# A deformable convolution's samples: 128x128 matmuls against two 64x64 tiles of TensorE

## The chip, the cores and the metric

The kernel runs on one core of one Trainium2 chip. The metric is the device time of one execution in microseconds (us); before the change three runs gave 6296.52 to 6303.05, median 6301.44.

## What is computed

Four layers follow one another on an array of 4 x 128 x 128 x 128 in fp32. Each adds its result to its input, and each input is group-normalised first. The change is in the first, a deformable 3x3 convolution with four groups of 32 channels:

```python
offset = jnp.einsum('bchw,oc->bohw', x, w_off) + b_off[None, :, None, None]
...
py = off[:, :, :, 0] + (ky - PAD).reshape(1, 1, K * K, 1, 1) + jnp.arange(H, dtype=jnp.float32).reshape(1, 1, 1, H, 1)
...
val = gather(y0i, x0i) * (wy0 * wx0)[:, :, None]
val = val + gather(y0i, x0i + 1) * (wy0 * wx1)[:, :, None]
val = val + gather(y0i + 1, x0i) * (wy1 * wx0)[:, :, None]
val = val + gather(y0i + 1, x0i + 1) * (wy1 * wx1)[:, :, None]
wg = w.reshape(COUT, G, CG, K * K)
return jnp.einsum('bgckhw,ogck->bohw', val, wg)
```

For every output pixel, group and tap, an offset of its own moves the place that the tap reads; the value there is a bilinear mix of four pixels. The other three layers (a scan of 1-D convolutions over rows, a message layer, a triangle product) are not touched.

## The kernel before, in words

`deform_layer` works on blocks of 3 output rows (RY), 43 per image, 172 in all. Within a block, columns are taken 4 at a time (RX): 32 column blocks. The kernel relies on offsets smaller than one pixel in size (a general version stands by for larger ones and isn't run here), so, with each tap counted at the place that it looks at, the samples around 3 x 4 places all lie in a patch of 5 x 6 = 30 pixels (NS). A bilinear mix is then a product: samples = patch x weights, where the weight of a patch pixel is a tent in y times a tent in x.

The partition dimension of that product carries 4 groups x 30 pixels = 120 lanes (LANES). The patch, `pixels`, is a block-diagonal matrix: lanes of group g have values in the 32 channels of group g alone, zeros elsewhere (the tiles are cleared once, before the loops, and the loads write only the diagonal). Three steps make one block:

- `spread_offsets` (L465, matmul L488): the two tents of every lane, from offsets split into three bf16 parts. `spread` holds the stationary matrices, 25 rows x LANES columns, for 10 phases. They stand four times, at partitions 0, 32, 64 and 96, so that these matmuls run on tiles of 32 rows x 128 columns. One tap takes 9 matmuls (three rows of 130 columns for y, six for x of 96 or 3 columns); taps come in pairs, 5 slots per block (SLOTS), into the PSUM tiles `t_ps`.
- `tents` (L494): ScalarE copies the y half out of PSUM (L497), VectorE multiplies it with the x half into `m` (L498), fp32, LANES x 9 taps x 3 rows x 130 columns.
- `sample` (L500, matmul L507): for each of four column blocks, `pixels` is stationary (120 x 128, fp32) and 27 rows of 4 columns of `m` are moving, 108 columns; the result, 128 channels x 108, goes to `v_ps`. `keep_samples` copies four of them at a time to `v` (L518). The last column block has two columns more (162).

`convolved` (L556, matmul L567) then applies the 3x3 taps as 15 matmuls of 128x128 weights over 128 to 384 columns, accumulating in `conv_ps`; `finish` (L540) adds the input and stores.

All orders are written by hand: `manual_schedule` (L656) makes each engine run its instructions in the order in which the code issues them. A block's loop has 8 steps (L676 to L689), and in each TensorE gets: lane matmuls of the next block if the table DONE asks for them (5 of 8 steps), two or three matmuls of the convolution (7 of 8), four sample matmuls, and a piece of side work from `step` (transposes L365 and offset matmuls L380 for rows that come later). Lane matmuls use 32-row tiles; everything else uses the whole array.

Loads stand on SP's queue: `load_places` (offsets), `load_pixels` (L453, four per block, one for each group, each 30 partitions), and x for the side work. The end block of each image has an extra row, done with narrow samples (`me`, 12 columns).

An fp32 matmul is two weight loads and two passes on TensorE; the profile counts each.

Of the kernel before, what the change touches and what calls it, by code (L numbers as in the profile page):

```python
# [21 lines left out]
NG = 4  # L22
NK = 9
NL = NK * NG
CG = P // NG
# [13 lines left out]
RY, RX = 3, 4  # L39
SY, SX = RY + 2, RX + 2  # L40
NS = SY * SX
LANES = NS * NG
NXB = S // RX
NG_X = NXB // 4
NYB = S // RY + 1
# [137 lines left out]
def deform_layer(tc, c, small, x, w_off, b_off, w_def, x1, tabs, offs):  # L183
# [9 lines left out]
    nc = tc.nc  # L193
# [3 lines left out]
    with ExitStack() as ctx:  # L197
# [22 lines left out]
        NPY, NPX = RY + 1, RX + 2  # L220
        NPH = NPY + NPX
        spread = wp.tile([P, NPH, LANES], BF16, name="spread")
        nc.vector.memset(spread, 0.0)
# [11 lines left out]
        with tc.tile_pool(name="l0prep", bufs=1) as prep:  # L235
            mask = prep.tile([NG, LANES], F32, name="mask")
            nc.vector.memset(mask, 1.0)
            nc.gpsimd.affine_select(
                out=mask, in_=mask, pattern=[[1, LANES]], compare_op=ALU.is_ge,
                fill=0.0, base=0, channel_multiplier=-NS,  # L240
            )
            nc.gpsimd.affine_select(
                out=mask, in_=mask, pattern=[[-1, LANES]], compare_op=ALU.is_ge,
                fill=0.0, base=NS - 1, channel_multiplier=NS,
            )
            awayi = prep.tile([NG, NPH, LANES], I32, name="awayi")
            for i in range(NPY):
                nc.gpsimd.iota(
                    awayi[:, i], pattern=[[0, NG], [1, SY], [0, SX]], base=-1 - i,
                    channel_multiplier=0,  # L250
                )
            for i in range(NPX):
                nc.gpsimd.iota(
                    awayi[:, NPY + i], pattern=[[0, NG * SY], [1, SX]], base=-1 - i,
                    channel_multiplier=0,
                )
            away = prep.tile([NG, NPH, LANES], F32, name="away")
            nc.vector.tensor_copy(away, awayi)
            at = {}
            for v in (-1, 0, 1):  # L260
                at[v] = prep.tile([NG, NPH, LANES], F32, name=f"at_{v + 1}")
                nc.vector.tensor_scalar(at[v], away, float(v), None, ALU.is_equal)
            kinds = prep.tile([NG, 3, NPH, LANES], F32, name="kinds")
            nc.vector.tensor_tensor(kinds[:, 0], at[0], at[-1], ALU.subtract)
            nc.vector.tensor_tensor(kinds[:, 1], at[1], at[-1], ALU.add)
            nc.vector.scalar_tensor_tensor(
                kinds[:, 1], at[0], -2.0, kinds[:, 1], ALU.mult, ALU.add
            )
            for i in range(2):
                nc.vector.tensor_tensor(  # L270
                    kinds[:, i], kinds[:, i],
                    mask.unsqueeze(1).to_broadcast([NG, NPH, LANES]), ALU.mult,
                )
            nc.vector.tensor_copy(kinds[:, 2], at[0])
            kinds16 = prep.tile([NG, 3, NPH, LANES], BF16, name="kinds16")
            nc.vector.tensor_copy(kinds16, kinds)
            for q in range(4):
                p0 = 32 * q
                nc.sync.dma_start(spread[p0 : p0 + 1], kinds16[0:1, 2])
                for g in range(NG):  # L280
                    for kind in range(2):
                        for n in range(NSPLIT):
                            p1 = p0 + 1 + g * NPART + kind * NSPLIT + n
                            nc.sync.dma_start(spread[p1 : p1 + 1], kinds16[g : g + 1, kind])


            zrow = prep.tile([NXB, 2 * SX * P], F32, name="zrow")
            nc.vector.memset(zrow, 0.0)
            zoff = prep.tile([2 * NL, NPART, 2 * OW], BF16, name="zoff")
            nc.vector.memset(zoff, 0.0)  # L290
            for b in range(B):
                t = tabs[b].rearrange("x (r s) c -> x r s c", s=SX)
                nc.scalar.dma_start(
                    t[0:NXB, 0:2].rearrange("x r s c -> x (r s c)"), zrow
                )
                nc.scalar.dma_start(
                    t[0:NXB, S + 2 : S + 3].rearrange("x r s c -> x (r s c)"), zrow[:, 0 : SX * P]
                )
                for r0 in range(0, S, NXB):
                    nc.scalar.dma_start(  # L300
                        t[0:1, 2 + r0 : 2 + r0 + NXB, 0:2].rearrange("x r s c -> (x r) (s c)"),
                        zrow[:, 0 : 2 * P],
                    )
                rows_ = offs[b].rearrange("(p n) l -> p n l", n=NPART)
                nc.scalar.dma_start(rows_[:, :, 0 : 2 * OW], zoff)
                nc.scalar.dma_start(rows_[:, :, (S + 2) * OW :], zoff)
# [146 lines left out]
        def load_pixels(b, j):  # L453
            t = pixels[(b * NYB + j) % 2]
            for g in range(NG):
                nc.sync.dma_start(
                    t[g * NS : (g + 1) * NS, :, g * CG : (g + 1) * CG],
                    tabs[b][0:NXB, RY * SX * j : RY * SX * j + NS, g * CG : (g + 1) * CG].rearrange(
                        "x l c -> l x c"
                    ),  # L460
                )
            return t
# [37 lines left out]
        def sample(m, pix, i, rows):  # L500

            n = rows * RX
            vp = ps_v.tile([P, 4 * n + 2 * rows], F32, name="v_ps")
            for h in range(4):
                xb = 4 * i + h
                w = RX + 2 if xb + 1 == NXB else RX
                nc.tensor.matmul(  # L507
                    vp[:, h * n : h * n + rows * w].rearrange("p (k c) -> p k c", c=w),
                    lhsT=pix[0:LANES, xb, :], rhs=m[:, :, RX * xb : RX * xb + w],
                    start=True, stop=True,  # L510
                )
            return vp

        def keep_samples(vp, v, i, rows):
# [144 lines left out]
        load_row(0)  # L659
        load_row(1)  # L660
        pixel_tiles = {0: load_pixels(*blocks[0])}
        for i in range(NB_):
            multiply(advance(i + 1))
        vps, before, convs, stats = None, None, iter(()), None
        for n, (b, j) in enumerate(blocks):
            load_row(n + 2)
            if n + 1 < len(blocks):
                pixel_tiles[n + 1] = load_pixels(*blocks[n + 1])
            pix = pixel_tiles.pop(n)
            m = ms.pop(n).rearrange("p k r c -> p (k r) c")  # L670
# [47 lines left out]
        while step(B, S):  # L718
# [10 lines left out]
            most_ps, lhsT=most, rhs=c.ident[0 : 2 * NL, 0 : 2 * NL], start=True, stop=True  # L729
# [852 lines left out]
@with_exitstack  # L1582
def tile_preact_convs(ctx: ExitStack, tc: tile.TileContext, x, w_off, b_off, w_def, w_conv,
                      wself_T, wm_T, wk_T, *rest):
    nc = tc.nc
    *w3, out = rest
    cpool = ctx.enter_context(tc.tile_pool(name="consts", bufs=1))
    small = ctx.enter_context(tc.tile_pool(name="small", bufs=1))
    dram = ctx.enter_context(tc.tile_pool(name="dram", bufs=1, space=DRAM))
    c = make_consts(nc, cpool)  # L1590
    imgs = [
        dram.tile([PADW * NG * PADW, 4 * CG], F32, name=f"img_{b}") for b in range(B)
    ]
    tabs = [dram.tile([NXB + 1, (S + 3) * SX, P], F32, name=f"tab_{b}") for b in range(B)]
    offs = [
        dram.tile([2 * NL * NPART, (S + 4) * OW], BF16, name=f"off_{b}") for b in range(B)
    ]
    x1 = dram.tile([B, S, S, S], F32, name="x1")
    x2T = dram.tile([B, P, S, S], F32, name="x2T")
    x3d = dram.tile([B, P, S, S], F32, name="x3d")  # L1600
    gates = dram.tile([B, P, S, S], F32, name="gates")
    norms, far = deform_layer(tc, c, small, x, w_off, b_off, w_def, x1, tabs, offs)
    with tc.If(nc.values_load(far, min_val=0, max_val=1) > 0):
        deform_general(tc, c, norms, x, w_off, b_off, w_def, x1, imgs)
    counted = scan_layer(tc, c, small, x1, w_conv, norms, x2T)
    message_and_triangle(tc, c, x2T, x3d, gates, counted, (wself_T, wm_T, wk_T), w3, out)
# [45 lines left out]
```

## Time and profile before

| what | value |
|---|---|
| median of three runs | 6301.44 us |
| the profiled execution's own time | 6289.25 us |
| its span, first to last instruction | 6287.5 us |
| mean granted TensorE clock | 0.934 |
| first and last sample matmul (L507) | 222.7 and 3753.4 us |
| sample matmuls, `m` / `me` | 11,008 / 256 passes |
| lane matmuls L488 | 14,016 weight loads |
| convolution L567 | 5,160 passes |

PE is TensorE's matmul row and PEld its weight-load row; loads overlap matmuls, and the recorded duration of a matmul includes its latency, so the distance from one start to the next says more of the pace than the duration does. DVE is VectorE, ACT ScalarE, POOL GpSimd, SP the engine that issues most DMAs. In a group line the columns are: line, engine, operation, tiles and shapes, count, busy us, mean ns of one, idle us before it and what ended that idle time. A form such as 120*128 is the stationary operand, rows by columns. PEclk is the granted share of TensorE's clock in tenths.

### The profile page before, as it was taken

How to read it: one execution, taken by the hardware profiler on the slowest of the kernel's cores; microseconds unless marked ns; L12 is line 12 of the kernel's file. 1: busy time of each engine (PE TensorE's matmuls, PEld its weight loads, DVE VectorE, ACT ScalarE, POOL GpSimd, SP SyncE). 2: the span in 40 equal slices, each digit the busy share in tenths (PEclk: the TensorE clock that was granted, in tenths of full speed). 3: DMA queues.
4: the chain of work that ended last, by engine and by line, in shares of the span. 5: the costliest groups of instructions: out<-in, count | busy, mean ns of one | idle time of the engine just before them, and what ended most of it. 6: DMA issues, size and time to landing. Idle time of an engine off the chain costs nothing. (4 is left out here: it accounts for less than half of the span.)

```text
span 6287.5 us, 117915 instructions
## 1 busy us (share of the span) xinstructions
PE 5392.4 (86%) x45160; PEld 4669.4 (74%) x45160; DVE 3346.1 (53%) x10388; ACT 2803.2 (45%) x5848; POOL 762.4 (12%) x660
## 2 busy tenths in 40 slices
PE   0588999899898998989999998999879679688697
PEld 0477878788777787777888888999838458466586
DVE  5353434354344454443333338999964665656656
ACT  0334444344444444444444432333254574564655
POOL 0111111001111101111000001222200100200102
PEclk9989999899999999999999998999989899899898
DMA  2445545445454444545333422323230521612514
GB/s 88 103 123 118 122 112 122 111 102 126 113 115 117 102 123 118 117 113 117 80 71 74 79 54 85 95 84 92 81 141 29 216 102 46 223 54 91 196 45 153
DMA packets 1112274, 668.36 MB, mean 106 GB/s; under 512 B 718933, under 2 KB 985366, under 8 KB 1095318
## 3 DMA queue, kind: packets, MB, share of 16 engines
q1 hardware_dynamic: 1101906, 655.37, 38.7%
q8 instruction: 361, 5.91, 0.4%
q10 hardware_dynamic: 9796, 5.34, 0.3%
q14 instruction: 211, 1.73, 0.1%
HBM read 380.24 MB, written 280.03 MB: 105 GB/s over the span
## 5 line engine op out<-in xcount | busy, mean ns | idle before, releaser
L498 DVE TENSOR_TENSOR m<-ty,t_ps 120x390 f32<-120x390 f32 x1548 | 804.8, 557 | 1788.2 <-ACT ty L497 1787.7
L507 PEld LDWEIGHTS v_ps<-m,pixels 120*128 120x128 f32 x11008 | 1439.0, 199 | 86.8 <-issue 12.0
L507 PE MATMUL v_ps<-m,pixels 120*128 120x108 f32 (+1 forms) x11008 | 1484.8, 280 | 2.6 <-ACT v L523 1.7
L567 PE MATMUL conv_ps<-v,wdef 128*128 128x128 f32 (+2 forms) x5160 | 1336.6, 386 | 12.1 <-DVE x1c L540 7.6
L518 ACT COPY v<-v_ps 128x432 f32<-128x432 f32 x1376 | 704.0, 512 | 1331.3 <-PE v_ps L507 1329.0
L567 PEld LDWEIGHTS conv_ps<-v,wdef 128*128 128x128 f32 x5160 | 834.1, 197 | 172.5 <-issue 28.9
L497 ACT COPY ty<-t_ps 120x390 f32<-120x390 f32 x1560 | 686.0, 486 | 376.1 <-PE t_ps L488 367.6
L488 PEld LDWEIGHTS <-spread 25*120 25x120 bf16 x14016 | 500.9, 143 | 266.0 <-issue 199.5
L488 PE MATMUL t_ps<-places,spread 25*120 25x96 bf16 (+2 forms) x13932 | 582.2, 247 | 83.3 <-DVE m L498 62.7
L1429 PEld LDWEIGHTS proj_ps<-wcat,X 128*128 128x128 f32 x4096 | 474.5, 192 | 27.4 <-issue 27.4
L1429 PE MATMUL proj_ps<-wcat,X 128*128 128x128 f32 x4096 | 483.8, 275 | 0.6
L386 POOL TENSOR_TENSOR off<-off,koff 72x512 f32<-72x512 f32 x128 | 162.1, 1267 | 2538.8 <-DVE off L383 2510.2
L1047 PE MATMUL m_ps<-carry,w 128*128 128x172 f32 x2286 | 361.3, 310 | 0.0
L1034 ACT ACTIVATE rowT<-x1T_ps,t_x,s_x 128x128 f32<-128x128 f32 x512 | 192.7, 457 | 366.4 <-PE x1T_ps L1027 363.6
L1510 POOL TENSOR_TENSOR work<-work,gate 128x512 f32<-128x512 f32 x128 | 165.0, 1293 | 1571.6 <-ACT work L1509 1435.2
L1047 PEld LDWEIGHTS m_ps<-carry,w 128*128 128x128 f32 x2286 | 345.5, 188 | 0.0
L1435 DVE TENSOR_TENSOR L<-proj_ps,work 128x256 f32<-128x256 f32 x256 | 155.0, 606 | 347.9 <-ACT work L1433 347.9
L1114 POOL TENSOR_TENSOR sum_h<-sum_h,x2c 128x512 f32<-128x512 f32 x128 | 162.6, 1270 | 1351.8 <-DVE x2c L1111 1351.8
L1433 ACT ACTIVATE work<-proj_ps 128x512 f32<-128x512 f32 x256 | 152.8, 597 | 298.1 <-PE proj_ps L1429 298.1
L365 PE MATMUL img_ps<-ident,xin 128*128 128x128 f32 x512 | 94.2, 315 | 196.2 <-DMA xin<-in_x_dram 193.4
L1522 PE MATMUL out_ps<-outw,work 128*128 128x128 f32 x1024 | 210.0, 307 | 48.9 <-POOL work L1510 48.7
L1518 PE MATMUL out_ps<-ident,x3cols 128*128 128x128 f32 x512 | 154.9, 303 | 92.8 <-DMA x3cols<-x3d 92.7
(230 smaller groups left out, 6805.3 us busy)
## 6 DMA issues: line engine op xcount, KB each, us to landing
pixels<-tab SPq DMA_DIRECT2D x688, 120.0 KB
xin<-in_x_dram SPq DMA_DIRECT2D x56, 1024.0 KB
off<-parts SPq DMA_DIRECT2D x64, 891.0 KB
tab<-rows SPq DMA_DIRECT2D x384, 128.0 KB
places<-off SPq DMA_DIRECT2D x688, 55.7 KB
x<-x1c SPq DMA_DIRECT2D x32, 1024.0 KB
x1rows<-x SPq DMA_DIRECT2D x128, 256.0 KB
x2T<-x2c SPq DMA_DIRECT2D x128, 256.0 KB
```

The lines of the kernel that those rows point to most:

```text
L488: nc.tensor.matmul(to, lhsT=spread[p0 : p0 + KROWS, ph, :], rhs=mov, start=True, stop=True,)
L497: nc.scalar.copy(ty[:, 0:n], tp[0:LANES, 0, 0:n])
L498: nc.vector.tensor_tensor(m, ty[:, 0:n], tp[0:LANES, 1, 0:n], ALU.mult)
L507: nc.tensor.matmul(vp[:, h * n : h * n + rows * w].rearrange("p (k c) -> p k c", c=w), lhsT=pix[0:LANES, xb, :], rhs=m[:, :, RX * xb : RX ...
L518: nc.scalar.copy(v[:, :, c0 : c0 + full * RX].rearrange("p k (h c) -> p k h c", c=RX), vp[:, 0 : full * n].rearrange("p (h k c) -> p k h c ...
L567: nc.tensor.matmul(pc[:, at : at + r1 - r0, :], lhsT=wdef[:, 3 * ky + kx, :], rhs=v[:, k0 + kx, r0:r1, kx : kx + S], start=m == 0, stop=m ...
L1034: nc.scalar.activation(rt[:, b, :], px[:, b, :], AF.Identity, bias=t, scale=s)
L1047: nc.tensor.matmul(to, lhsT=wgt, rhs=src[:, :, at : at + n], start=i == 0, stop=i + 1 == len(todo),)
L1114: nc.gpsimd.tensor_tensor(sum_h, sum_h, x2c[:, :, i], add)
L1429: nc.tensor.matmul(pp[:, j], lhsT=X[:, j0 + j, :], rhs=wcat[:, cols], start=True, stop=True)
L1510: nc.gpsimd.tensor_tensor(a, a, gt, ALU.mult)
L1522: nc.tensor.matmul(po[:, j], lhsT=a[:, j], rhs=outw, start=False, stop=True)
```

## The change

The lanes of a group get a pitch of 32 instead of 30, so that LANES is 128 and two groups fill exactly 64 partitions. The two lanes between groups have tents of zero: `mask` is zero there, and `awayi` holds 64, a distance at which no tent is 1. `load_pixels` writes each group at its new pitch. A sample matmul is replaced by two: groups 0 and 1 (partitions 0 to 63, channels 0 to 63) on one 64x64 tile of TensorE, groups 2 and 3 on the other, both into the same `v_ps` at their own partitions. Lane matmuls keep their form, with 128 instead of 120 weight columns. The convolution, side work and all orders stay.

```diff
--- before.py
+++ after.py
@@ -39,7 +39,8 @@
 RY, RX = 3, 4
 SY, SX = RY + 2, RX + 2
 NS = SY * SX
-LANES = NS * NG
+LG = 32
+LANES = LG * NG
 NXB = S // RX
 NG_X = NXB // 4
 NYB = S // RY + 1
@@ -237,21 +238,28 @@
             nc.vector.memset(mask, 1.0)
             nc.gpsimd.affine_select(
                 out=mask, in_=mask, pattern=[[1, LANES]], compare_op=ALU.is_ge,
-                fill=0.0, base=0, channel_multiplier=-NS,
+                fill=0.0, base=0, channel_multiplier=-LG,
             )
             nc.gpsimd.affine_select(
                 out=mask, in_=mask, pattern=[[-1, LANES]], compare_op=ALU.is_ge,
-                fill=0.0, base=NS - 1, channel_multiplier=NS,
+                fill=0.0, base=NS - 1, channel_multiplier=LG,
             )
             awayi = prep.tile([NG, NPH, LANES], I32, name="awayi")
+            nc.gpsimd.memset(awayi, 64)
+
+            def lanes(i):
+                return awayi[:, i].rearrange("p (g s) -> p g s", s=LG)[:, :, 0:NS].rearrange(
+                    "p g (y x) -> p g y x", x=SX
+                )
+
             for i in range(NPY):
                 nc.gpsimd.iota(
-                    awayi[:, i], pattern=[[0, NG], [1, SY], [0, SX]], base=-1 - i,
+                    lanes(i), pattern=[[0, NG], [1, SY], [0, SX]], base=-1 - i,
                     channel_multiplier=0,
                 )
             for i in range(NPX):
                 nc.gpsimd.iota(
-                    awayi[:, NPY + i], pattern=[[0, NG * SY], [1, SX]], base=-1 - i,
+                    lanes(NPY + i), pattern=[[0, NG], [0, SY], [1, SX]], base=-1 - i,
                     channel_multiplier=0,
                 )
             away = prep.tile([NG, NPH, LANES], F32, name="away")
@@ -454,7 +462,7 @@
             t = pixels[(b * NYB + j) % 2]
             for g in range(NG):
                 nc.sync.dma_start(
-                    t[g * NS : (g + 1) * NS, :, g * CG : (g + 1) * CG],
+                    t[g * LG : g * LG + NS, :, g * CG : (g + 1) * CG],
                     tabs[b][0:NXB, RY * SX * j : RY * SX * j + NS, g * CG : (g + 1) * CG].rearrange(
                         "x l c -> l x c"
                     ),
@@ -504,11 +512,12 @@
             for h in range(4):
                 xb = 4 * i + h
                 w = RX + 2 if xb + 1 == NXB else RX
-                nc.tensor.matmul(
-                    vp[:, h * n : h * n + rows * w].rearrange("p (k c) -> p k c", c=w),
-                    lhsT=pix[0:LANES, xb, :], rhs=m[:, :, RX * xb : RX * xb + w],
-                    start=True, stop=True,
-                )
+                for at in (slice(0, 2 * LG), slice(2 * LG, 4 * LG)):
+                    nc.tensor.matmul(
+                        vp[at, h * n : h * n + rows * w].rearrange("p (k c) -> p k c", c=w),
+                        lhsT=pix[at, xb, at], rhs=m[at, :, RX * xb : RX * xb + w],
+                        start=True, stop=True,
+                    )
             return vp
 
         def keep_samples(vp, v, i, rows):
```

## The prediction

> **What bounds the kernel now.** I read the page's busy shares first, then busy time by stretches, then TensorE's waits, the groups by line, and last TensorE's timeline in one stretch at full clock.
>
> ```profile
> PE 5392.4 (86%) x45160; PEld 4669.4 (74%) x45160; DVE 3346.1 (53%) x10388; ACT 2803.2 (45%) x5848; POOL 762.4 (12%) x660
> ...
> PEclk9989999899999999999999998999989899899898
> ```
>
> The stretches (columns: PE, PEld, DVE, ACT, POOL busy, granted clock, DMA share, GB/s) cut out the deformable layer, whose sampling runs from 222 to 3753 us:
>
> ```profile
> 200.00:600.00 400.00, 315.25 (x2767) 267.49 (x2767) 175.64 (x593) 155.31 (x331) 60.13 (x54) 0.88 0.48 120
> 600.00:3500.00 2900.00, 2695.18 (x25921) 2338.21 (x25920) 1220.81 (x3436) 1357.17 (x2929) 354.14 (x318) 0.94 0.47 108
> 3500.00:3770.00 270.00, 262.68 (x2572) 233.76 (x2570) 89.46 (x273) 116.31 (x263) 0.00 (x0) 0.97 0.33 67
> ```
>
> In the middle stretch TensorE is busy for 93%, VectorE for 42%, ScalarE for 47%. The rest is mostly one wait, a load of x in front of the transposes:
>
> ```profile
> PE img_ps L365 <- DMA xin<-in_x_dram: 193.4, 29, 12.4
> PE t_ps L488 <- DVE m L498: 62.7, 39, 8.6
> ```
>
> So in these 3,570 us TensorE sets the end, and what it gains or loses comes back nearly whole. The groups that the change touches:
>
> ```profile
> L507 PEld LDWEIGHTS v_ps<-m,pixels 120*128 120x128 f32 x11008 | 1439.0, 199 | 86.8 <-issue 12.0
> L507 PE MATMUL v_ps<-m,pixels 120*128 120x108 f32 (+1 forms) x11008 | 1484.8, 280 | 2.6 <-ACT v L523 1.7
> L488 PEld LDWEIGHTS <-spread 25*120 25x120 bf16 x14016 | 500.9, 143 | 266.0 <-issue 199.5
> L488 PE MATMUL t_ps<-places,spread 25*120 25x96 bf16 (+2 forms) x13932 | 582.2, 247 | 83.3 <-DVE m L498 62.7
> ```
>
> 5,504 fp32 matmuls of L507 stand as 11,008: each is two weight loads with two passes over the same 108 columns. The 199 and 280 ns are latencies; the pace is read from starts (start, duration, line):
>
> ```profile
> 3601.65 0.48 PE L567 MATMUL conv_ps<-v,wdef 128*128 128x384 f32 x1
> 3601.98 1.04 PE L507 MATMUL v_ps<-m,pixels 120*128 120x108 f32 x8
> 3602.95 0.62 PE L488 MATMUL t_ps<-places,spread 25*120 25x130 bf16 x18
> 3603.50 1.34 PE L567 MATMUL conv_ps<-v,wdef 128*128 128x384 f32 x4
> 3604.68 1.04 PE L507 MATMUL v_ps<-m,pixels 120*128 120x108 f32 x8
> 3605.65 0.61 PE L488 MATMUL t_ps<-places,spread 25*120 25x130 bf16 x9
> 3606.19 1.13 PE L567 MATMUL conv_ps<-v,wdef 128*128 128x256 f32 x4
> ...
> 3611.04 1.04 PE L507 MATMUL v_ps<-m,pixels 120*128 120x108 f32 x8
> 3611.93 0.29 PE L567 MATMUL conv_ps<-v,wdef 128*128 128x128 f32 x1
> ```
>
> Five prices follow. (a) Eight sample passes take 0.89 us when the convolution follows: 112 ns each. (b) A pass of 384 columns takes 0.33 us, 0.85 ns a column, so 108 columns stream in 92 ns: the 112 are set by loading 128 weight columns, not by the stream. (c) When the lane matmuls of L488 follow, the same eight take 0.97: seven at 112, 92 of stream, 95 ns over. TensorE empties before it goes from the whole array to tiles of 32 rows. (d) Going back, the four passes of 256 columns at 3606.19 take 0.97 for 0.87 of streams: 0.10 us, a weight load that nothing covers. (e) Eighteen lane matmuls on four row tiles take 0.55, nine on two of them 0.54: tiles on different rows do run at once.
>
> **What the Trainium skill says.**
> - "TensorEngine Tiling (Array Packing)", Key Properties: changing the tiling mode drains TensorE, changing the tile alone doesn't. (c) and (e) agree, for 32x128 against 128x128. No run here shows 64x64.
> - "TensorE: Matmul & The Clock Gate", LDWEIGHTS: a load's time goes by its columns (columns/1.2 ns, 107 for 128), not its rows. (a) agrees; 64 columns should take about 56.
> - The same page, Part 3, The mechanism: loads overlap running matmuls of other row groups, while matmuls start and end strictly in order. (e) shows the first half.
> - The same page, Weight-path perf modes: loads of exactly 128 columns, not fp32, are read faster, measured about 2x. The spread loads go from 120 to 128 columns, and in the compiled program they turn into four pieces of 32. The trace of before has no such load.
>
> **The change, part by part.** Order on every engine is unchanged; only sizes and the number of sample matmuls change.
>
> *Sample passes.* They become 22,016, with 64 columns of weights, on two disjoint tiles. Program order is tile 0 pass 1, pass 2, then tile 1 pass 1, pass 2. In-order starts let pass 2 of tile 0 run beside pass 1 of tile 1, and pass 2 of tile 1 beside the next block's pass 1; two passes of one tile can't overlap. Four passes thus cost two streams and the few ns between starts (about 4 on the page cited for the mechanism), 2 x 92 + 5 = 189 against 224 now, and each run of sample passes ends with one stream alone. 5,504 x 0.189 + 1,237 runs x 0.092 = 1,154 us against 11,008 x 0.112 = 1,233. Where lanes follow (710 times) the last pass of before is already counted at 92, 14 us less. Net **-65 us**. From both sides: if streams overlap perfectly at 90, -95; if the 27 short rows of four elements slow the stream to 105 ns (nothing separates this from the load now, and L488's strided 96 columns are its only relative), about +85.
>
> *Mode switches.* Today the samples share the convolution's mode. I counted runs of one mode in the built order: 863 into 32-row tiles and 863 back, 1,726 in all. Afterwards there are 1,237 entries into 64x64, 1,371 into the whole array (convolutions, transposes, offsets) and 863 into 32-row tiles, 3,471 in all. That is 1,745 more drains; at 0.095 from (c), rounded to 0.105 since the other direction shows no separate number, **+183 us** (0.09 to 0.12: 157 to 209).
>
> *Exposed loads.* After a drain the first load has no cover: 508 more whole-array entries at 0.107, from (d), **+54**; 1,237 entries into 64x64 at half of (a), 0.056, **+69**.
>
> *Lanes.* Matmul widths are unchanged. In each of 863 phases the first load is exposed, and two 3-column passes are too short to hide theirs: about 55 ns saved per phase if loads halve, **-50 us** (a load of 120 columns estimated at 50 ns, since bf16 needs half of fp32's passes). Without the fast load, 8 more columns cost +6; at a quarter, -70.
>
> *Nothing else.* The ScalarE copy and VectorE product of lanes have 128 partitions instead of 120 with the same 390 elements each, so the same time; at 47% and 42% busy neither becomes the bound even if they grew by a twentieth. Four pixel loads per block move the same bytes from the same SP queue to other partitions; if partition placement slowed them, the x load's stall would grow, at most a fifth of 193 us. POOL's extra memset of 4x1280 and its iotas run in the first 200 us, where POOL is busy for 20; bounded by 2 us. No wait is added: tile 0 needs two of the four pixel loads, tile 1 the rest, and both products already need all of m.
>
> *Sum:* -65 + 183 + 54 + 69 - 50 = +191 on TensorE. The 32 narrow sample calls of the end blocks, load-bound, go from 256 passes at 112 to 512 at 56: no change. In the stretch from 200 to 600 us, 11% of the layer, TensorE is only 79% busy, so some 10 may vanish. The profiled execution took 6289 us (span 6287.5), 12 below the median of the runs: 6289 + 191 - 10 + 12 = 6482. The uncertain stream leans upward, so I forecast **6500 us**.
>
> **Rivals.**
> 1. *The tiles work, the drain doesn't come between 64x64 and 128x128.* Prefetching survives there: the switches (183) and loads (54 + 69) go, leaving samples and lanes, -65 - 50 = -115: about **6190**, and up to 6340 with the slow stream. Against it: (c) shows the drain on this chip for another pair of modes and the page states it generally. For it: no run shows this pair. It decides from the point where drains and exposed loads come to less than 115 us together, three eighths of the 306 that I count.
> 2. *The tiles don't overlap* (fp32's two passes, or the shared PSUM bank). Then 22,016 streams of 92 run in line: 2,025 instead of 1,154, +871 on my sum: about **7355**. (e) speaks against it, though with one pass per matmul.
> 3. *The change doesn't do what it says*: the loads aren't what paces samples. Then 64 columns bring nothing, samples stay at 224 per block, +190 for 35 x 5,504: 6690, inside the main case's upper end.
>
> **Numbers.** Main case, with rival 3 in its upper end: 0.63, own range 6400 to 6720. Rival 1: 0.21. Rival 2: 0.12. Something else, either sign: 0.04. The range reaches from 6190, rival 1, to 6720 and leaves out rival 2. About 0.2% is what a measurement of this kernel can tell from no change. Faster: three quarters of rival 1 and half of the rest, 0.18; within: 0.03; slower: 0.79.
>
> **What would show it.** In the profile after: sample passes x22016 at starts averaging 47 to 52 ns; a gap of about 0.15 us between the convolution's last stream and the first sample pass, and 0.2 between the last sample pass and a convolution; lane phases of 0.49 instead of 0.54; the layer's end near 3,960 instead of 3,765; later layers unchanged. I am wrong if conv-to-sample shows no gap, if four passes take 370 ns, or if VectorE, ScalarE or the pixel loads become what TensorE waits for.

## The result, and the profile after

The changed kernel takes 6310.97 us, median of 13 runs, against 6296.26 for the kernel before, also 13 runs: ratio 1.0024, 95% interval 1.0016 to 1.0033. I had forecast 6500, so the direction is right and the size is not: +15 us in place of +200. The profiled execution took 6317.03 us, its span is 6315.3. It was the slowest of its 13, and the profiled execution of before was about as fast as the fastest of those 13, so the two profiles lie 28 us apart, not 15.

Busy shares and granted clock of the changed kernel:

```profile
PE 5418.1 (86%) x56424; PEld 4315.0 (68%) x56424; DVE 3348.6 (53%) x10388; ACT 2787.1 (44%) x5848; POOL 763.4 (12%) x661
...
PEclk9989999899999999999999998999979899899898
```

Weight loads are 354 us less busy, matmuls 26 us more; the other engines, and the clock in this pair of profiles, are about as before. The stretches of the deformable layer:

```profile
200.00:600.00 400.00, 313.31 (x3708) 230.32 (x3708) 174.95 (x592) 154.00 (x331) 60.05 (x54) 0.88 0.47 120
600.00:3500.00 2900.00, 2689.51 (x34820) 2024.46 (x34820) 1212.37 (x3418) 1331.10 (x2897) 353.75 (x318) 0.94 0.46 108
3500.00:3790.00 290.00, 289.32 (x3980) 224.93 (x3977) 93.47 (x254) 128.98 (x296) 0.00 (x0) 0.98 0.33 65
```

The layer's last convolution matmul starts at 3793 us instead of 3764, and the later layers take as long as before. In the groups, sample passes have doubled in number and shrunk in sum, and both lane rows have fallen:

```profile
L516 PE MATMUL v_ps<-m,pixels 64*64 64x108 f32 (+1 forms) x22016 | 1379.4, 267 | 4.7 <-ACT v L527 3.3
...
L516 PEld LDWEIGHTS v_ps<-m,pixels 64*64 64x64 f32 x22016 | 1091.4, 135 | 351.9 <-issue 205.3
...
L496 PEld LDWEIGHTS <-spread 25*128 25x128 bf16 x14016 | 437.7, 105 | 296.2 <-issue 207.3
L496 PE MATMUL t_ps<-places,spread 25*128 25x96 bf16 (+2 forms) x13932 | 525.4, 235 | 81.7 <-DVE m L506 62.5
```

TensorE's timeline, in the same stretch as in the prediction:

```profile
3602.02 0.98 PE L516 MATMUL v_ps<-m,pixels 64*64 64x108 f32 x16
3602.93 0.55 PE L496 MATMUL t_ps<-places,spread 25*128 25x130 bf16 x9
3603.41 1.13 PE L576 MATMUL conv_ps<-v,wdef 128*128 128x256 f32 x4
3604.47 1.83 PE L516 MATMUL v_ps<-m,pixels 64*64 64x108 f32 x32
3606.24 0.56 PE L496 MATMUL t_ps<-places,spread 25*128 25x130 bf16 x18
...
3608.22 0.98 PE L516 MATMUL v_ps<-m,pixels 64*64 64x108 f32 x16
3609.13 0.71 PE L576 MATMUL conv_ps<-v,wdef 128*128 128x128 f32 x4
```

Read it from one start to the next. The convolution's four passes of 256 columns, 0.97 us before, now take 1.06 until the samples start: the drain that I had counted is there, 0.09. Sixteen sample passes take 0.91, with lanes or the convolution behind them. Take away 0.09 for the drain at their end and 0.055 for their first load, which nothing covers, and 0.76 is left: eight times 95 ns, so the passes run in pairs with none left over. I had counted nine. A lane phase takes 0.48 instead of 0.54. The first hundredths of the long run show the pairing, from matmuls and from loads:

```profile
3604.47 0.31 PE L516 MATMUL v_ps<-m,pixels 64*64 64x108 f32 x2
```

```profile
3604.47 0.20 PEld L516 LDWEIGHTS v_ps<-m,pixels 64*64 64x64 f32 x4 [0.33 <-issue]
```

Two passes have begun and four loads are under way before 0.09 us have gone: both tiles start at once, though the second tile's first pass is third in the program. (The trace doesn't name the tile of a pass. I read it from the spacing: in e3, below, where one tile's passes come first, they start singly, 95 ns apart.)

To split the layer I added up, in each trace, the distances from one matmul's start to the next between the first sample and the last convolution matmul; distances over 0.9 us I count as waits, the others as TensorE's own sum. Before: 3,259 us of its own and 282 of waits. After: 3,275 and 296. So TensorE itself takes 17 us more and waits 13 more, together 30 of which the rest of the program takes 2 back. These sums come from one profile each, and the limit is a choice: with 0.7 us the difference of TensorE's own is 7, with 1.2 it is 22.

### The profile page after: what moved, and what is told of

It reads as the page before. It is cut to its first block, busy times and chain, and to the rows that moved or that the text cites. A ratio compares the mean times of both kernels' runs of the same rounds, so it can differ in the third digit from the quotient of the medians.

```text
span 6315.3 us, 140614 instructions
## 1 busy us (share of the span) xinstructions
PE 5418.1 (86%) x56424; PEld 4315.0 (68%) x56424; DVE 3348.6 (53%) x10388; ACT 2787.1 (44%) x5848; POOL 763.4 (12%) x661
## 5 line engine op out<-in xcount | busy, mean ns | idle before, releaser
L506 DVE TENSOR_TENSOR m<-ty,t_ps 128x390 f32<-128x390 f32 x1548 | 805.0, 557 | 1817.0 <-ACT ty L505 1816.0
L516 PE MATMUL v_ps<-m,pixels 64*64 64x108 f32 (+1 forms) x22016 | 1379.4, 267 | 4.7 <-ACT v L527 3.3
L576 PE MATMUL conv_ps<-v,wdef 128*128 128x128 f32 (+2 forms) x5160 | 1366.2, 393 | 12.5 <-DVE x1c L549 7.4
L516 PEld LDWEIGHTS v_ps<-m,pixels 64*64 64x64 f32 x22016 | 1091.4, 135 | 351.9 <-issue 205.3
L505 ACT COPY ty<-t_ps 128x390 f32<-128x390 f32 x1560 | 687.6, 489 | 363.2 <-PE t_ps L496 351.4
L496 PEld LDWEIGHTS <-spread 25*128 25x128 bf16 x14016 | 437.7, 105 | 296.2 <-issue 207.3
L496 PE MATMUL t_ps<-places,spread 25*128 25x96 bf16 (+2 forms) x13932 | 525.4, 235 | 81.7 <-DVE m L506 62.5
```

Of the source, the lines that this page charges most:

```text
L496: nc.tensor.matmul(to, lhsT=spread[p0 : p0 + KROWS, ph, :], rhs=mov, start=True, stop=True,)
L505: nc.scalar.copy(ty[:, 0:n], tp[0:LANES, 0, 0:n])
L506: nc.vector.tensor_tensor(m, ty[:, 0:n], tp[0:LANES, 1, 0:n], ALU.mult)
L516: nc.tensor.matmul(vp[at, h * n : h * n + rows * w].rearrange("p (k c) -> p k c", c=w), lhsT=pix[at, xb, at], rhs=m[at, :, RX * xb : RX * ...
L576: nc.tensor.matmul(pc[:, at : at + r1 - r0, :], lhsT=wdef[:, 3 * ky + kx, :], rhs=v[:, k0 + kx, r0:r1, kx : kx + S], start=m == 0, stop=m ...
```

## The experiments

Theory A, formed from this trace: samples gain about 190 us and lanes 58, and mode switches with the loads that they uncover give some 285 back. Rivals: B, TensorE's order and prices are as I predicted and something else fell in my favour; C, waits for loads of x made the result. All ratios are against the kernel before, which ran again beside each of these.

**e1: the pitch alone.** Samples stay on the whole array.

```diff
-                for at in (slice(0, 2 * LG), slice(2 * LG, 4 * LG)):
-                    nc.tensor.matmul(
-                        vp[at, h * n : h * n + rows * w].rearrange("p (k c) -> p k c", c=w),
-                        lhsT=pix[at, xb, at], rhs=m[at, :, RX * xb : RX * xb + w],
...
+                nc.tensor.matmul(
+                    vp[:, h * n : h * n + rows * w].rearrange("p (k c) -> p k c", c=w),
+                    lhsT=pix[:, xb, :], rhs=m[:, :, RX * xb : RX * xb + w],
```

> Pitch of 32 and 128 lanes, but each sample stays one matmul on the whole array (128x128). Theory A (the change gains on sample passes, about 190 us, and on lanes, 58 us, and gives some 285 us back in mode switches and the weight loads that they uncover): only the lanes' gain is left, with no new switch: 6238 us against 6296 before, a lane phase of 0.48 us instead of 0.54, sample passes still 112 ns apart. Rival B (128 lanes save nothing, the changed kernel's near balance comes from switches that cost half of what I counted): 6296 us, or 6301 for eight more columns per load.

6245.89 us, 0.9921 (0.9900 to 0.9941). TensorE's sum 3,195, 63 less than before; waits 292. Its timeline:

```profile
3602.49 1.34 PE L575 MATMUL conv_ps<-v,wdef 128*128 128x384 f32 x4
3603.67 1.04 PE L515 MATMUL v_ps<-m,pixels 128*128 128x108 f32 x8
3604.64 0.56 PE L496 MATMUL t_ps<-places,spread 25*128 25x130 bf16 x9
3605.12 1.13 PE L575 MATMUL conv_ps<-v,wdef 128*128 128x256 f32 x4
```

Eight sample passes take 0.97 ahead of lanes, as before, and the lane phase 0.48. The lanes' gain comes without the tiles, and the change without its last part, the two sample matmuls, is 1% faster than with it.

**e2: two tiles, without the fast load.**

```diff
+USED = LANES - LG + NS
...
-                            to, lhsT=spread[p0 : p0 + KROWS, ph, :], rhs=mov,
+                            to, lhsT=spread[p0 : p0 + KROWS, ph, 0:USED], rhs=mov,
```

> The changed kernel with 126 instead of 128 columns in each lane weight load (the last two lanes carry nothing; the copy, the product and the second tile's rows end at lane 126). Theory A, with the fast load of exactly 128 columns as the source of the lanes' gain: lane phases go back from 0.48 to 0.54 us, 863 of them, +50 to +58 us: 6365 us. Rival (the lanes' gain comes from the mode that now precedes them, 64x64 tiles in place of the whole array, or from the pitch): 6311 us, phases stay at 0.48.

6373.29 us, 1.0128 (1.0107 to 1.0149): 62 us above the changed kernel by the medians, TensorE's sum 3,330, 55 above. The lane rows are back where they were:

```profile
L497 PEld LDWEIGHTS <-spread 25*126 25x126 bf16 x14016 | 509.1, 146 | 292.5 <-issue 209.6
L497 PE MATMUL t_ps<-places,spread 25*126 25x96 bf16 (+2 forms) x13932 | 585.0, 249 | 82.8 <-DVE m L507 63.9
```

A load of 126 columns is recorded at 146 ns, one of 128 at 105. These durations include latency; the pace is seen at the head of a lane phase, where the second load on a tile starts 52 ns after the first with 120 columns, 54 with 126 and 15 with 128. The lanes' gain is the load of exactly 128 columns, as the Trainium skill has it ("TensorE: Matmul & The Clock Gate", Weight-path perf modes); neither pitch nor mode explains it.

**e3: one tile after the other.** The loop over `at` stands outside the loop over `h`, so that eight passes of tile 0 come before the first of tile 1.

```diff
-            for h in range(4):
-                xb = 4 * i + h
...
-                for at in (slice(0, 2 * LG), slice(2 * LG, 4 * LG)):
+            for at in (slice(0, 2 * LG), slice(2 * LG, 4 * LG)):
+                for h in range(4):
+                    xb = 4 * i + h
```

> The changed kernel with the sample matmuls of a step in another order: all four column blocks on tile 0, then all four on tile 1, so eight passes in a row stand on one tile before the first on the other. Theory A (each tile takes its passes from the queue by itself, so a pass may start ahead of an older one of the other tile): same overlap, 6311 us, 16 passes in about 0.76 us of streams. Rival B (passes start strictly in program order, as my prediction had it; only neighbours in the order can overlap): one pass of the first tile beside one of the second per step, 15 streams instead of 8, 7 x 95 ns x 1376 steps = +915 us: 7225 us.

6804.54 us, 1.0807 (1.0784 to 1.0830): +493 against the changed kernel, neither 0 nor 915. One run of samples, first what had started by 3604.715, then by 3604.73, then the whole run and the group behind it:

```profile
3604.28 0.59 PE L516 MATMUL v_ps<-m,pixels 64*64 64x108 f32 x4
```

```profile
3604.28 0.75 PE L516 MATMUL v_ps<-m,pixels 64*64 64x108 f32 x6
```

```profile
3604.28 1.41 PE L516 MATMUL v_ps<-m,pixels 64*64 64x108 f32 x16
3605.63 1.56 PE L576 MATMUL conv_ps<-v,wdef 128*128 128x384 f32 x4
```

Four passes start alone, then two within 15 ns. The single starts in the trace say it in full: tile 0 starts its eight passes from 0 to 720 ns; tile 1 starts its first at 442, 6 ns after tile 0's fifth, while tile 0's sixth to eighth still wait. Then both run together for four passes, and tile 1 finishes alone: 12 streams instead of 8. So a pass does overtake older passes of the other tile, here three of them. Such a run of 16 takes 1.34 us up to the next group instead of 0.91: four streams of 95 ns and 0.05 for tile 1's first load. TensorE's sum rose by 584 us and the waits fell by 84, which leaves about the 493. Strict order of starts is refuted, and full independence of the tiles too.

**e7: two column blocks per tile in turn**, to test that limit of three.

> The changed kernel with two column blocks in a row on tile 0, then two on tile 1: four passes of one tile ahead of the first of the other. From e3, where the second tile's first pass started beside the fifth of the first tile's eight: a pass may overtake up to three waiting passes of the other tile. Then nothing changes here: 6311 us. If it may overtake only one (all that the changed kernel itself needs), tile 1 starts after the third pass: up to two streams more per run of samples, 1237 x 2 x 0.095 = +235 us: 6546 us.

The edit:

```diff
+            for at, h in (
+                (slice(64 * d, 64 * d + 64), 2 * pair + k)
+                for pair in range(2) for d in range(2) for k in range(2)
+            ):
```

6359.70 us, 1.0103 (1.0080 to 1.0125): +49 against the changed kernel, neither the 0 nor the 235 that I expected. Sixteen passes take 0.96 instead of 0.91:

```profile
3603.40 1.03 PE L518 MATMUL v_ps<-m,pixels 64*64 64x108 f32 x16
3604.36 0.71 PE L578 MATMUL conv_ps<-v,wdef 128*128 128x128 f32 x4
```

By the single starts the tiles begin together and keep step for five pairs, 13 ns apart, so overtaking three works. At the sixth pair one tile falls 52 to 58 ns behind, once per run and for the rest of it. That is about the load of 64 columns (55 ns), so I take it that the pass was let ahead and its load came late; this is argued from the size alone. It isn't a stream: 1,237 runs at 0.05 are 62 us, and TensorE's sum rose by 51. What sets the limit at three is open.

**e4: fewer switches.** The convolution is issued only in steps with lanes.

```diff
-                next(convs, None)
+                if i in (0, 2, 3, 5, 6, 7):
+                    next(convs, None)
...
-                convs = convolved(b, *terms_of(j, before, v), stats, 3, 2)
+                convs = convolved(b, *terms_of(j, before, v), stats, 3, 3)
```

> The changed kernel with the convolution's 15 matmuls dealt out three at a time, and only in the five of eight steps that have lane matmuls; in two of the other three steps the sample passes then follow those of the step before with nothing between. Built order: 951 instead of 1219 entries from the whole array into 64x64, 266 instead of 537 back. Theory A, with 0.092 us per switch and 0.055 and 0.107 for the uncovered loads: 268 x 0.147 + 271 x 0.199 = 93 us less: 6218 us, below both kernels. Rival C (switches cost little; the gain went into the wait for x in front of the transposes): 6311 us or more, that wait grown above 197 us.

**e5: the same order with the samples of e1**, where it saves no switch.

> The order of e4 (convolution three at a time, only where lanes are) with the samples of e1, on the whole array: samples and convolution share one mode, so the new order saves no switch (863 entries into 32-row tiles, as in e1). Theory A (e4 won by its fewer switches): no gain over e1, 6246 us, within about 10. Rival (e4 won by the order itself, for instance by less waiting for the convolution's accumulator or for x): 88 us below e1, 6158 us.

e4: 6222.72 us, 0.9885 (0.9863 to 0.9907), 88 below the changed kernel. e5: 6216.23 us, 0.9880 (0.9861 to 0.9899), 30 below e1 by the medians, about 26 by the ratios with some 18 of uncertainty. So e4 came within 5 us of its number partly by luck: about 26 of the 88 come from the order itself. In TensorE's sums the order gives 20 (3,195 to 3,175), all in the distances after lane matmuls, and e4 120 (3,275 to 3,155). The remaining 100 agree with the 93 of the switches, but e4's waits rose by 27. In the lane part the work is as long in e5 as in e1 (0.49 us for a phase of 18); what went are short gaps behind a phase's second start, over 0.11 us 140 times in e1 and 38 in e5. What TensorE waited for there is open.

**e8: more switches.** Half of a step's convolution goes between the samples' second and third column block.

```diff
+                if h == 2 and halfway:
+                    halfway()
...
-                vps = sample(m, pix, i, NK * RY), vk, i, NK * RY
+                vps = sample(m, pix, i, NK * RY, lambda: next(convs, None)), vk, i, NK * RY
```

> The changed kernel with more mode switches and no other work: each step's piece of the convolution is cut in two, the second standing between the second and the third column block of the samples. Built order: 2395 instead of 1219 entries into 64x64 from the whole array, 1716 instead of 537 back. Theory A, with 0.147 and 0.199 us for the two kinds: +173 + 235 = +408 us: 6719 us. Rival (the switch is partly covered by other work, or its price comes once per step): clearly less, 6311 to 6500 us.

6646.02 us, 1.0555 (1.0531 to 1.0579): +335 instead of +408. TensorE's sum says +392 (3,667), 96% of the price; the waits fell by 49. Three groups of its timeline, in which eight sample passes take 0.54 us, four pairs at 95 ns, 0.055 and 0.09, and its wait for x (us, times, longest):

```profile
3603.04 0.49 PE L578 MATMUL conv_ps<-v,wdef 128*128 128x128 f32 x2
3603.45 0.60 PE L518 MATMUL v_ps<-m,pixels 64*64 64x108 f32 x8
3603.99 0.49 PE L578 MATMUL conv_ps<-v,wdef 128*128 128x128 f32 x2
```

```profile
PE img_ps L373 <- DMA xin<-in_x_dram: 160.1, 29, 11.2
```

There are 1,179 more switches out of the 64x64 tiles and 1,179 more into them, so 392 us make 0.333 for one of each, against 0.147 + 0.199 = 0.346. That confirms the two prices' sum, not each of them. The wait for x, 197 us in the changed kernel, is 160 here, which is most of the 49, presumably because TensorE comes later to the transposes while the load takes as long as before.

**e6: the side work beside the convolution**, on top of e4, and **e9: the same with the lanes' copy and product issued first.**

```diff
+                multiply(todo)
+                for _ in range(2 if ready[b] < min(S, RY * j + 26) else 1):
+                    step(b, RY * j + 2)
                 vps = sample(m, pix, i, NK * RY), vk, i, NK * RY
```

(In e6 `multiply` stays behind `sample`.)

> e4, and the side work (transposes and offset matmuls for later rows) placed right after the convolution's matmuls instead of after the samples, so that it shares their mode: 101 instead of 266 entries from 64x64 into the whole array. Theory A: 165 x 0.199 = 33 us below e4: 6190 us. Rival C (the wait for x rules here): no gain, 6223 us or more, since the transposes now ask for x earlier after its load was issued.

> e6, with the lanes' copy and product issued ahead of the side work instead of behind it; TensorE's order is that of e6. e6 spared 33 us of switches, but TensorE waited 108 us for VectorE's lane product where it had waited 83 in e4, because that product stood behind the side work on VectorE's queue. Theory A: that wait goes back to about 80 us and the spared switches show, 25 us below e6: 6188 us. Rival (the placing of the side work delays TensorE in another way, through ScalarE's copies or the loads of x): no change, 6213 us.

e6: 6212.62 us, 0.9874 (0.9853 to 0.9895). e9: 6225.61, 0.9890 (0.9872 to 0.9907). Neither can be told from e4 or from the other, so the 6190 and 6188 that I expected didn't come. What TensorE waits for in e4, e6 and e9, in that order:

```profile
PE img_ps L373 <- DMA xin<-in_x_dram: 209.8, 29, 13.0
PE t_ps L496 <- DVE m L506: 82.7, 75, 9.4
```

```profile
PE img_ps L373 <- DMA xin<-in_x_dram: 203.1, 29, 13.5
PE t_ps L496 <- DVE m L506: 107.8, 110, 9.1
```

```profile
PE img_ps L373 <- DMA xin<-in_x_dram: 233.6, 29, 13.1
PE t_ps L496 <- DVE m L506: 73.1, 74, 7.5
```

In e6 TensorE's sum fell by only 7 us (3,155 to 3,148), and its wait for VectorE's product rose by 25. e9 took that wait back (73 us), and the sum fell to 3,129, but the wait for x rose by 30. Here rival C has its part: this wait takes back a share of what TensorE gains.

**e10, e11, e12: that wait away**, in the kernel before, the changed one, and e9. Seven pieces of the side work's schedule, instead of one, lie between the load and the transposes.

```diff
             nc.sync.dma_start(xc, x[b, :, y0 : y0 + RC, :])
-            yield
+            for _ in range(7):
+                yield
```

> The kernel before, with seven pieces' time instead of one between the load of x for the side work and the transposes that need it, so that TensorE no longer waits for it (193 us in the profile of before). If that wait is real room on TensorE: 190 us less, 6107 us. If the load is only moved behind other loads, or the side work then comes too late for the blocks: 6200 us or more.

> The changed kernel with the same. Theory A: without the wait for x, the two kernels differ by TensorE's own sum alone, which the traces put at +17 us (3275 against 3259): 15 to 20 us above e10, 6124 us. Rival C (the wait for x hid or made part of the difference): the distance to e10 is clearly another, below 5 or above 35 us.

> e9 with the same. In e9 TensorE's own sum fell by 19 us against e6 and by 146 against the changed kernel, but its wait for x rose to 234 us and took most of the last step back. Theory A with that wait gone: 130 us below e10, which is the difference of TensorE's own sums (3129 against 3259): 5980 us, the fastest version. Rival (VectorE or ScalarE sets the pace by then): less than 70 us below e10.

In this order they took 6036.52 us (0.9582, 0.9568 to 0.9595), 6045.08 (0.9597, 0.9582 to 0.9612) and 5954.18 (0.9446, 0.9433 to 0.9459). The wait, in e10 and e11:

```profile
PE img_ps L366 <- DMA xin<-in_x_dram: 13.3, 1, 13.3
```

```profile
PE img_ps L374 <- DMA xin<-in_x_dram: 14.4, 2, 13.8
```

Both kernels gain the same, and e11 stays 9 us above e10 (the intervals overlap), with 3,194 against 3,181 us in TensorE's sums, 13 more. So in time the wait neither made nor hid the change's small loss. The clock hid some of it: the trace has TensorE at half clock for 181 us of the layer in e10 and for 133 in e11. Counting what lies in these stretches at half, the sums are 3,107 and 3,147, 41 apart. e12 is 82 below e10 where I expected 130; its sum is 3,083, 99 below, and 23 of that went into other waits. It is the fastest version here, 5.5% below the kernel before.

## Why the prediction was wrong

The sum was +191 on TensorE; the trace has +17. By its terms, where "measured" is a count from the traces times a price from the traces, for the lanes and the narrow samples the distances themselves:

| step | forecast, us | measured, us |
|---|---|---|
| sample passes | -65 | -173 |
| drains | +183 | +162 |
| uncovered loads, whole array and 64x64 | +54 +69 | +40 +68 |
| lanes | -50 | -58 |
| narrow samples | 0 | -22 |
| sum | +191 | +17, TensorE's sum +17 |

- **The step that failed is the one in the sample passes: "In-order starts let pass 2 of tile 0 run beside pass 1 of tile 1 ... and each run of sample passes ends with one stream alone."** The stream was right (95 ns for my 92 and 5 between tiles), and four passes in two streams was right. But the second tile needn't wait for the first one's second pass; it starts with the first, so no run has a stream left over. The term 1,237 x 0.092, 114 us, doesn't exist: 11,008 pairs x 0.095 is 1,046 us against 1,219. It is the largest part of the 174 us by which the sum was off; the rest is the narrow samples (22), the drains (21), the loads (15) and the lanes (8). e3 and e7 show how far the overtaking goes, three passes. I had taken strict order from the Trainium skill ("TensorE: Matmul & The Clock Gate", Part 3, The mechanism: matmuls start and end strictly in order), and nothing in the trace of before tested it, since its lane matmuls alternate between tiles and no overtaking was needed. Here page and measurement differ, and the measurement decides: between two 64x64 tiles, starts don't keep the program's order (the ends in a trace are modelled, so they can't be judged).
- **The same step hid the narrow samples' gain.** I put 512 loads at 56 ns in a row. But two tiles' passes start together here too; the distances after the narrow passes add up to 21 us where they took 44.
- **Drains** were right in kind and 13% high: after the changed kernel's streams the gap is 92 ns in both directions and for all three modes (conv to samples, samples to lanes, samples to conv, lanes to conv). 3,480 - 1,724 = 1,756 switches in the traces x 0.092 = 162. What the Trainium skill states ("TensorEngine Tiling (Array Packing)", Key Properties) holds for 64x64 too; e4 and e8 priced drain and uncovered load together by taking switches away and adding them.
- **Uncovered loads**: the trace has 55 ns before the second sample pass and 107 to 109 before the second convolution pass, as forecast. But of 537 entries from samples into the whole array only 277 go to the convolution. Before a second transpose or offset matmul it is 55 to 58, so these entries cost about 40 us, not 54.
- **Lanes**: 58 for 50. My estimate of a load of 120 columns, 50 ns, was good (52), but the fast one takes 15, not half of it. e2 gives 55 of the 58 back, so the fast load is nearly the whole.
- **Group by group.** Both programs issue the same groups in the same order, so each can be set beside its partner: samples with their own uncovered loads and drains -54 us, convolution +141, lanes -58, narrow samples -23, the side work with the rest +11, together +17. This supports the table. That its sum agrees to the microsecond is chance: its prices are those of full clock, and counted at full clock TensorE's sums are 3,097 and 3,119, 23 apart.
- **Around the sum.** The 6500 stood 18 us above the sum's own 6482. The profile's further 13 us are waits, put at nothing. So was the clock, and it may have helped: over 13 executions of the changed kernel it was 0.934 to 0.937, over 40 of the kernel before, beside the experiments, 0.929 to 0.936 with a median of 0.932, while the profiled pair has 0.934 twice. How much of the step from 28 to 15 us is the clock was not tried.
- **Rivals.** 1 fell (drains are there), 2 fell (tiles overlap), 3 fell: passes went from 112 to 95 ns per stream. The likeliest case had drains, uncovered loads and the fast load right in kind; it had the order of starts wrong, which made a term of 114 us that doesn't exist. The right direction owes something to luck: +15 is what is left of gains and losses of over 250 us each. My own both-sided bounds covered the stream's length, but not the order of starts, and that is why the case's own range of 6400 to 6720 missed.

## What to carry to other kernels

Here a finer tile gained only between two switches of mode, and each switch emptied TensorE (92 ns) and uncovered a load (55 to 109 ns). So put work of one mode together before making tiles smaller, and count the runs in the built order. When a trace can't show whether a queue is strict, that is an unknown cost like any other: bound it from both sides. And look for what a change does on its way: here the padding to 128 columns, which only made room for the tiles, was worth 51 us alone, while the tiles on top of it lost 65 (e1 against the changed kernel).

## What the runs showed of the hardware that I had not expected

- A pass of one 64x64 tile overtakes up to three waiting passes of the other tile (e3: the second tile's first pass starts with the fifth of eight; e7: with four of one tile first in the program, both tiles' first passes start 13 ns apart).
- A load of 128 bf16 columns is recorded at 105 ns, one of 126 at 146, one of 120 at 143: two columns more are faster (e2). By the starts of two loads on one tile it is 15 ns against 54 and 52.
- A wait costs TensorE more than its length. In the middle stretch, without the wait for x, the granted clock rose from 0.94 to 0.98:

```profile
600.00:3400.00 2800.00, 2595.18 (x24880) 2249.09 (x24878) 1185.26 (x3344) 1308.12 (x2821) 354.14 (x318) 0.94 0.47 109
```

```profile
600.00:3400.00 2800.00, 2756.60 (x27411) 2400.25 (x27408) 1275.19 (x3589) 1425.79 (x3085) 357.66 (x321) 0.98 0.51 116
```

The first line is the kernel before, the second e10. TensorE's own sum fell from 3,259 to 3,181 with the same work, so some 180 us of waiting, once gone, gave 262 us from profile to profile. The clock accounts for the difference: the traces have TensorE at half clock for 437 us of the layer in before and for 181 in e10. A convolution pass of 256 columns takes 216 ns at full clock and 427 in these stretches. Of TensorE's own sum 324 and 149 us lie in them; counted at half, the sums are 3,097 and 3,107, so all of the 78 us is the clock. That the waits bring on the half clock follows from e10 and e11, where nothing but the load's lead was changed; how long a wait has to be for it was not tried.
